# Cross-attention's output projections of eight tiles in pairs, by seven half products, in the turns after the batches are done

## The chip, the cores and the metric

The kernel runs on one core of a Trainium2 chip. The metric is device time of one execution in microseconds (us), lower is better; the median of several runs is given. PE is TensorE's matmuls, PEld its weight loads, DVE VectorE, ACT ScalarE, POOL GpSimd, SP the queue that issues the DMAs.

## The reference

One decoder block on x (8 batches x 224 tokens x 512) in float32, post-normalised, with a context of 8 x 750 x 384:

```python
x = layernorm(x + self_attention(x))        # 16 heads of 64
x = layernorm(x + cross_attention(x, ctx))  # below
x = layernorm(x + ffn(x))                   # ternary weights, inner 2048

# cross_attention
q, k, v = split(x @ Wq), split(ctx @ Wk), split(ctx @ Wv)
attn = softmax(q k^T * 64**-0.5)
out = merge(attn @ v)                       # 8 x 224 x 1024
return out @ Wo + bo                        # Wo: 1024 x 512
```

The change is in the last line alone: `out @ Wo`, a product of 1792 x 1024 by 1024 x 512, for 10 of its 14 tiles of 128 rows.

## The kernel before

x lies in SBUF as 14 tiles of 128 tokens x 512 (`x[0]` to `x[13]`). Three stages follow each other: self-attention to about 488 us of the span, cross-attention to about 1448, the feed-forward part to the end.

**Cross-attention** goes in 32 turns, `t` = 0 to 31, after a start turn -1. Eight turns make a group `p` of two batches (448 tokens); a turn takes four heads of one batch: `place(t)` gives group, head quarter `g` and batch `u`, odd turns are the second batch. So a group's tokens are complete, over all heads, at the end of the turn after its eighth. In a turn PE does, in this order:

1. `weighted(t - 1)`: softmax weights of the turn before times V (`ov_c`, L1383);
2. `scores(t)`: `sc_c` (L1253), 12 banks, in two halves `w` of two heads; ACT copies them out (L1235), DVE takes maxima (L1239);
3. `kv_steps(t, 1)` and `kv_steps(t + 1, 0)`, interleaved: V of this turn and K of the next (L1084, L1078);
4. `queries_opened` or `queries_closed`, the query products of the next pair of turns (L1091);
5. in some turns `cross_project` of the tiles that are complete: `project_out` (L264), eight matmuls of 128 x 128 by 128 x 512 into one bank (`mm_co`).

Beside this DVE finds each query's largest score in `maxima(w)` and subtracts it in `less_maxima` (L1355); ACT takes exponentials (L1367); POOL sums them for the denominators (`exponentials`, L1370 to L1372); DVE normalises the outputs of the turn before into `oT` (`normalise`, `coT`, L1326). `oT` is a ring of 512 tokens.

K, V and query products already use Strassen-Winograd: a product of 2 x 2 blocks by seven products of blocks instead of eight, with sums of blocks on POOL. Its sums of weights are prepared in self-attention in a tile `room` on POOL and stored to DRAM (`room_sums`, `room_query_sums`, called in self-attention turns 10 to 23), and are loaded again for each turn.

`done` says after which turn each tile's projection comes: tile 0 after turn 7, 1 and 2 after 8, 3 and 4 after 15, 5 and 6 after 16, 7 after 23, 8 and 9 after 24, the others after 31 and at the end. `cross_add` adds the bias on POOL (L1399), the bank on DVE (L1400), and takes the layernorm statistics.

The engines' order (PE, DVE, ACT, POOL) is the order in which the program calls them; each engine takes its instructions in that order and waits where a semaphore asks it to. SP's order is the scheduler's. Products take their PSUM banks from one pool of seven (`ps_mm`), in turn. The tiles of the pool `sb` have one buffer each unless `bufs` says otherwise: a new tile of a name waits until every reader of the one before is done. `w_t` has two; it takes the rounded weights of the feed-forward part on their way to DRAM in turns 12 to 23.

Of the kernel before, what the change touches and what calls it, by code (L numbers as in the profile page):

```python
# [21 lines left out]
F32 = mybir.dt.float32  # L22
BF16 = mybir.dt.bfloat16
AF = mybir.ActivationFunctionType
ALU = mybir.AluOpType
# [29 lines left out]
QG = HEADS // 4  # L55
EARLY = 7
CROWDED = 0, 7
LATE = 10
SOFTCLAMP = 50.0
SCALE = DH**-0.5  # L60
# [7 lines left out]
def decoder_block(ctx: ExitStack, tc: tile.TileContext, a: dict, out: bass.AP):  # L68
# [97 lines left out]
    def room_query_load():  # L166
        nc.sync.dma_start(
            out=room.rearrange("p (k n) -> p k n", k=KD),
            in_=a["xattn_Wq"].rearrange("(k p) n -> p k n", p=P),
        )  # L170

    def room_query_sums():

        blk = room.rearrange("p (h k g c n) -> p h c k g n", h=2, k=2, c=2, n=P)
        b = lambda h, c: blk[:, h, c]
        for n, y, p, q in (
            (0, b(0, 0), b(0, 1), b(0, 0)),
            (2, b(0, 1), b(1, 1), b(0, 1)),
            (1, b(1, 1), b(1, 1), b(0, 0)),
            (3, b(1, 0), b(1, 0), b(1, 1)),  # L180
        ):
# [5 lines left out]
    room_steps = room_sums(0), room_sums(1), room_query_sums()  # L187

    ident = const.tile([P, P], F32, name="ident")
    make_identity(nc, ident)  # L190
# [156 lines left out]
    with tc.tile_pool(name="a_sb", bufs=2) as sb, tc.tile_pool(  # L347
# [418 lines left out]
        for m in range(NS):  # L766
# [26 lines left out]
                next(room_steps[m // 15])  # L793
            if 20 <= m < 24:
                next(room_steps[2])
            next(sums)
            if m + 2 < NS:
                square_qk(m + 2)
# [36 lines left out]
                room_load(1)  # L835
            if m == 18:
                room_query_load()
            if m == NS - 3:
# [100 lines left out]
    with tc.tile_pool(name="c_sb", bufs=1, reuse_waits="tile") as sb, tc.tile_pool(  # L939
# [4 lines left out]
        ctx_odd = sb.tile([P, CTX], F32, name="ctx_odd")  # L944
        for b in range(1, B):
            open_context(b, (ctx_even, ctx_odd)[b % 2])
        xwo = load_w("xattn_Wo", INNER // P, DIM)
        load_context(1)
        nc.sync.dma_start(out=bo, in_=a["xattn_bo"].partition_broadcast(P))
        stage = sb.tile([P, 2, CHUNK], F32, name="w_stage")  # L950
# [445 lines left out]
            )  # L1396

        def cross_add(i):
            nc.gpsimd.tensor_tensor(x[i], x[i], bo, ALU.add)  # L1399
            nc.vector.tensor_tensor(x[i], outs.pop(i), x[i], ALU.add)  # L1400
            statistics(x[i], ln_mv[:, i, :], ln_ve[:, i, :])

        TURNS = B // 2 * 2 * QG
        jobs = {}
# [4 lines left out]
        for t, i0, i1 in ((18, 0, EARLY), (26, EARLY, LATE)):  # L1409
            job(t, roots, i0, i1)  # L1410
            n = t + 1
            for i in range(i0, i1):
                job(n, normalise_x, nc.gpsimd, i)
                n += 1
                job(n + (i == LATE - 1), largest_x, i)
            if i1 < LATE:
                job(n, row_scales, i0, i1)
        job(28, quantise_x, 0)
        job(29, quantise_x, 1)

        done = {}
        for i in range(NX):
            b = ((i + 1) * P - 1) // S
            t = 2 * QG * (b // 2 + 1) - 2 + b % 2
            done.setdefault(t + 1, []).append(i)

        kts, vs, outs = {}, {}, {}
        pTs = prior = None
        transpose_x(0)
        sum_x()  # L1430
        for n in range(2):
            stage_chunk(*chunks[n], n)
        for t in range(-1, TURNS):
# [3 lines left out]
            if t >= 0:  # L1437
                pTs = scores(t, copy if t else None)
                if t == 0:
                    weight_open(t)  # L1440
                nm = maxima(0)
                less_maxima(nm, pTs[0])
                if t == TURNS - 1:
                    for _ in normalise(t - 1, ov):
                        pass
                nm = maxima(1)
            ks = kv_steps(t + 1, 0) if t + 1 < TURNS else iter(())
            vals = kv_steps(t, 1) if t >= 0 else iter(())
# [313 lines left out]
```

## Time and profile before

| | |
|---|---|
| median of 3 runs | 1601.79 us (1601.24 to 1602.21) |
| profiled execution | 1601.96 us, span 1600.1 us |
| PE busy | 99% of the span |
| DVE, ACT, POOL busy | 83%, 62%, 61% |
| granted TensorE clock, mean | 0.999 |
| a turn of cross-attention without `mm_co` | mostly 26.3 us (even) or 27.0 us (odd) |
| `mm_co` of one tile on PE | 6.87 us |
| idle of PE that the list of waits names | 3.8 us in all |

Lines of the timeline read: start in us, length, engine, line of the kernel, operation, output <- inputs, shapes, how many instructions; in brackets the engine's idle time before it and what ended it. A float32 matmul is two instructions on PE. Matmuls are pipelined, so a group's length runs past the start of the next; the pitch is read from starts. Lines of a table by stretches read: from and to, length, busy time and count of PE, PEld, DVE, ACT and POOL, granted clock (1.00 is full), share of the DMA engines, GB/s.

### The profile page before, as it was taken

What the parts mean: (1) busy time and instruction counts of PE and PEld (TensorE: products, weight loads), DVE (VectorE), ACT (ScalarE), POOL (GpSimd) and SP (SyncE); (2) the same over time, 40 slices, a digit from 0 to 9 for tenths busy, and PEclk for the clock granted to TensorE, in tenths of its full rate; (3) what the DMA queues carried; (4) which work ended last, traced back from release to release, by engine and by line L of the source; (5) the groups of instructions that cost most, each with busy time, mean ns of one, the idle gap of its engine ahead of it and who ended that gap; (6) DMA issues with size and microseconds to landing.
All of it is one profiled execution on the core that took longest, in us unless ns stands there. A gap on an engine that the chain in (4) does not pass through costs nothing.

```text
span 1600.1 us, 27156 instructions
## 1 busy us (share of the span) xinstructions
PE 1589.1 (99%) x9684; PEld 1138.8 (71%) x9698; DVE 1323.8 (83%) x2809; ACT 996.9 (62%) x1858; POOL 972.6 (61%) x891
## 2 busy tenths in 40 slices
PE   9999999999999999999999999999999999999998
PEld 6677666667747888876888876788876888864443
DVE  3999897889966798886799876798887898978877
ACT  5667555656525777764668765687764666646663
POOL 5886565666524656685466785467686466753344
PEclk9999999999999999999999999999999999999999
DMA  8115342433204313241122252223240111213343
GB/s 302 47 53 198 90 129 85 139 89 119 83 20 162 105 59 100 66 159 54 60 67 80 85 181 64 73 81 118 79 162 24 34 40 38 73 54 97 64 90 106
DMA packets 143111, 149.14 MB, mean 93 GB/s; under 512 B 41088, under 2 KB 109184, under 8 KB 142592
## 3 DMA queue, kind: packets, MB, share of 16 engines
q1 hardware_dynamic: 142832, 147.40, 29.8%
q8 instruction: 77, 1.26, 0.3%
q14 instruction: 58, 0.48, 0.1%
q10 hardware_dynamic: 144, 0.00, 0.0%
HBM read 119.85 MB, written 18.87 MB: 87 GB/s over the span
## 4 chain that ended last, share of the span: by engine, by line
PE 94%; DVE 3%; ACT 2%; issue 1%; DMA 0%; POOL 0%; SPq 0%; POOLq 0%; ACTq 0%; DVEq 0%
PE sc_c L1253 10%; PE ov_c L1383 9%; PE v_x L1084 7%; PE k_x L1078 6%; PE mm_o L672 6%; PE mm_co L264 6%; PE mm_f L1558 5%; PE mm_v L547 5%; PE q_x L472 5%; PE v_w L1084 5%; PE k_w L1078 5%; PE mq_x L1091 3%; PE sc_a L574 3%; PE ov_a L643 3%; PE v_z L1084 3%; PE q_w L472 3%
## 5 line engine op out<-in xcount | busy, mean ns | idle before, releaser
L1370 POOL TENSOR_TENSOR csh<-cpT 125x672 f32<-125x672 f32 x128 | 209.8, 1639 | 109.8 <-DVE cpT L1355 94.0
L202 POOL TENSOR_TENSOR nm_i<-nm_q,mhalf 128x28 f32<-128x28 f32 x32 | 158.0, 4936 | 82.4 <-DVE nm_q L522 82.1
L1355 DVE TENSOR_TENSOR cpT<-cpT,mx_b 125x1344 f32<-125x1344 f32 x128 | 192.6, 1545 | 2.8
L1235 ACT COPY cpT<-sc_c 125x448 f32<-125x448 f32 x384 | 173.9, 566 | 18.3 <-PE sc_c L1253 14.1
L1367 ACT ACTIVATE cpT<-cpT 125x1344 f32<-125x1344 f32 x128 | 168.5, 1328 | 11.2 <-DVE cpT L1355 10.7
L1253 PE MATMUL sc_c<-cq,ckT 64*125 64x224 f32 x1536 | 162.2, 358 | 0.1
L1253 PEld LDWEIGHTS sc_c<-cq,ckT 64*125 64x125 f32 x1536 | 147.3, 184 | 14.4 <-issue 10.3
L1383 PE MATMUL ov_c<-cpT,cv 125*64 125x224 f32 x1536 | 152.9, 355 | 0.2 <-ACT cpT L1367 0.2
L1115 POOL TENSOR_TENSOR cv<-cv,cvmu 125x384 f32<-125x384 f32 x32 | 31.9, 998 | 191.5 <-ACT cv L1114 185.7
L1383 PEld LDWEIGHTS ov_c<-cpT,cv 125*64 125x64 f32 x1536 | 107.6, 137 | 44.9 <-issue 8.8
L547 PE MATMUL mm_v<-wv,xnT 128*128 128x512 f32 x224 | 100.4, 592 | 0.0
L1558 PE MATMUL mm_f<-ternary,xqT 128*128 128x512 bf16 x435 | 97.8, 379 | 0.7
L264 PE MATMUL mm_co<-xattn_Wo,coT 128*128 128x512 f32 x224 | 98.5, 593 | 0.0
L284 ACT ACTIVATE pr<-sc_a 128x448 f32<-128x448 f32 (+1 forms) x118 | 57.1, 535 | 60.3 <-PE sc_a L574 60.1
L1239 DVE TENSOR_TENSOR xw<-sc_c,cpT 125x448 f32<-125x448 f32 x64 | 39.6, 619 | 64.0 <-PE sc_c L1253 64.0
L1371 POOL TENSOR_TENSOR csm<-csh 125x224 f32<-125x224 f32 x128 | 85.1, 665 | 10.0
L1372 POOL TENSOR_TENSOR csm<-csm,csh 125x224 f32<-125x224 f32 x128 | 84.6, 661 | 10.0
L598 DVE TRANSPOSE_TENSOR_REDUCE sm_q<-pr 128x28 f32<-128x896 f32 x64 | 70.6, 1103 | 18.7 <-ACT pr L284 18.4
L1263 ACT COPY ov_s<-ov_c 128x448 f32<-128x448 f32 x31 | 16.5, 533 | 111.5 <-PE ov_c L1383 111.5
L672 PE MATMUL mm_o<-attn_Wo,oT 128*128 128x512 f32 x192 | 84.6, 593 | 0.0
L1558 PEld LDWEIGHTS <-xqT 128*128 128x128 bf16 x448 | 43.8, 98 | 53.2 <-issue 0.6
L264 PEld LDWEIGHTS mm_co<-xattn_Wo,coT 128*128 128x128 f32 x224 | 41.9, 190 | 47.9 <-issue 45.5
(240 smaller groups left out, 3992.7 us busy)
## 6 DMA issues: line engine op xcount, KB each, us to landing
w_slot<-qk_sums SPq DMA_DIRECT2D x22, 512.0 KB, 3.6
xw<-w_sums SPq DMA_DIRECT2D x32, 320.0 KB, 2.9
xwq<-xq_sums SPq DMA_DIRECT2D x16, 512.0 KB, 4.2
w_stage<-w_gateT SPq DMA_DIRECT2D x16, 512.0 KB, 5.5
w_stage<-w_upT SPq DMA_DIRECT2D x16, 512.0 KB, 5.3
w_stage<-w_downT SPq DMA_DIRECT2D x16, 512.0 KB, 4.4
tern<-w_t SPq DMA_DIRECT2D x24, 256.0 KB, 2.7
ternary<-tern SPq DMA_DIRECT2D x3, 2048.0 KB, 8.0
```

Source lines behind the costliest of these rows:

```text
L264: nc.tensor.matmul(mm, lhsT=oT[:, k, c : c + P], rhs=w[:, k, :], start=(k == 0), stop=(k == NPAIR - 1),)
L547: nc.tensor.matmul(mm, lhsT=xnT[:, k, at : at + P], rhs=wv[:, k, c * 512 : (c + 1) * 512], start=(k == 0), stop=(k == KD - 1),)
L672: nc.tensor.matmul(mm, lhsT=joint[g][:, hp, :] if at < 0 else o[:, at : at + P], rhs=wo[:, hp, :], start=(hp == 0), stop=(hp == NPAIR - 1),)
L1078: nc.tensor.matmul(mm, lhsT=w, rhs=c, start=start, stop=True, skip_group_check=True)
L1084: nc.tensor.matmul(mm[:, t, :], lhsT=c[:, t * CT : (t + 1) * CT], rhs=w, start=start and t == 0, stop=True, skip_group_check=True,)
L1235: nc.scalar.copy(pT[:, j, 2 * c2 : 2 * c2 + 2, :], banks[c2][j])
L1253: nc.tensor.matmul(sc[j][:, i, :], lhsT=kT[h0 : h0 + DH, w, ct * CT : (ct + 1) * CT], rhs=cq[h0 : h0 + DH, t % 2, w], start=True, stop=True,)
L1355: nc.vector.tensor_tensor(pT[:, j], pT[:, j], nm[:CT, j] .rearrange("p (o q) -> p o q", o=1) .to_broadcast([CT, NCT, S]), ALU.add,)
L1367: nc.scalar.activation(pT[:, j], pT[:, j], AF.Exp)
L1370: nc.gpsimd.tensor_tensor(half, pT[:, j, 0:3], pT[:, j, 3:6], ALU.add)
L1383: nc.tensor.matmul(ov[h0 : h0 + DH, w, :], lhsT=v[:, ct, hq * DH : (hq + 1) * DH], rhs=pTs[w][:, j, ct, :], start=(ct == 0), stop=(ct == N ...
L1558: nc.tensor.matmul(mm, lhsT=xqTs[i][:, k, :], rhs=w[:, k, cols], start=(k == 0), stop=(k == KD - 1),)
```

## The change

Tiles 0 to 9 are no longer projected when they are complete but one to two turns later, in turns 9, 17 and 25. `PAIRED` names them by turn: pair (0, 1) and tile 2; pairs (3, 4) and (5, 6); pair (7, 8) and tile 9. Each pair is a product of 256 x 1024 by 1024 x 512, taken in two halves of 256 columns `s`; each half is 2 x 2 blocks (128 rows, 512 of the inner dimension, 128 columns) and goes by seven products of blocks, each four matmuls with 128 columns. The first half of the columns stands behind the scores, ahead of `maxima(1)` in DVE's queue; the second at the end of the turn, behind the queries and the third exponential, ahead of the fourth.

`sum_out` makes the sums of the activations on POOL (three operations of 512 columns in the first half, of which S3 replaces a block of `oT`, two in the second), into two `w_t` tiles. `out_pair` does the products; partial results go through ACT into `cku4` and `cvu2`, buffers that `kv_steps` uses too, and are added to x on DVE (from PSUM) and POOL (from SBUF). `out_single` does a single tile in a half of 256 columns. The weights' half is loaded by `load_out(s)`: two blocks and four sums, 2 MB, the other half as soon as one has been used; after turn 25 the whole weight, for the tiles 10 to 13, which stay as they were. The sums of weights are made in self-attention turns 25 to 28 in `room`. The bias is added ahead, at the end of turns 4 to 6, 12 to 15 and 20 to 22; the statistics come at the end of turns 9, 17, 25.

```diff
+PAIRED = ((0, 1), (2,)), ((3, 4), (5, 6)), ((7, 8), (9,))
+    def room_out_load():
+        nc.sync.dma_start(
+            out=room.rearrange("p (k n) -> p k n", k=NPAIR),
+            in_=a["xattn_Wo"].rearrange("(k p) n -> p k n", p=P),
+        )
+    def room_out_sums():
...
+        for n, y, p, q in (
+            (0, b(0, 0), b(0, 1), b(0, 0)),
+            (2, b(0, 1), b(1, 1), b(0, 1)),
+            (1, b(1, 1), b(1, 1), b(0, 0)),
+            (3, b(1, 0), b(1, 0), b(1, 1)),
+        ):
+            for i in range(2):
+                nc.gpsimd.tensor_tensor(y[:, i], p[:, i], q[:, i], ALU.subtract)
+                nc.sync.dma_start(out=sums_xo[:, i, n], in_=y[:, i])
+            yield
...
-        xwo = load_w("xattn_Wo", INNER // P, DIM)
+        def load_out(s):
+            src = a["xattn_Wo"].rearrange("(k p) n -> p k n", p=P)
+            if s is None:
+                nc.sync.dma_start(out=xwo, in_=src)
+                return
+            for c in range(2):
+                at = (2 * s + c) * P
+                nc.sync.dma_start(
+                    out=xo[:, 2 * c : 2 * c + 2].rearrange("p h k n -> p (h k) n"),
+                    in_=src[:, :, at : at + P],
+                )
+            nc.sync.dma_start(out=xo[:, 4:], in_=sums_xo[:, s])
+        load_out(0)
...
+        def sum_out(pair, s):
+            (a11, _), (a21, a22) = (out_blocks(i) for i in pair)
+            s1, s2 = sums_o[pair] = [
+                sb.tile([P, CHUNK], BF16, name="w_t", bufs=2)
+                .bitcast(F32)
+                .rearrange("p (k n) -> p k n", n=P)
+                for _ in range(2)
+            ]
+            if s == 0:
+                nc.gpsimd.tensor_tensor(a21, a11, a21, ALU.subtract)
+            nc.gpsimd.tensor_tensor(s2, a22, a21, ALU.subtract)
+            nc.gpsimd.tensor_tensor(s1, s2, a11, ALU.add)
+        def out_product(mm, c, w, start):
+            for k in range(4):
+                nc.tensor.matmul(
+                    mm, lhsT=c[:, k], rhs=w[:, k], start=start and k == 0, stop=True,
+                    skip_group_check=True,
+                )
+        def out_pair(pair, s, following):
...
+            parts = sb.tile([P, HALF + 9], F32, name="cku4")
+            m1, u2, u4 = (parts[:, i * P : (i + 1) * P] for i in range(3))
+            w0 = sb.tile([P, HALF + 9], F32, name="cvu2")[:, :P]
...
+            out_product(x_, a11, b11, True)
+            nc.scalar.copy(m1, x_)
+            out_product(z_, a12, b21, True)
+            plus(nc.vector, c11, z_)
+            out_product(x_, s2, t2, False)
+            nc.scalar.copy(u2, x_)
+            nc.gpsimd.tensor_tensor(s2, a12, s2, ALU.subtract)
+            out_product(w_, s3, t3, True)
+            nc.scalar.copy(w0, w_)
+            out_product(x_, s1, t1, False)
+            nc.scalar.copy(u4, x_)
+            plus(nc.gpsimd, c11, m1)
+            out_product(w_, a22, t4n, False)
+            plus(nc.vector, c21, w_)
+            out_product(x_, s2, b22, False)
+            plus(nc.vector, c12, x_)
+            if following:
+                sum_out(following, s)
+            for y, q in ((c22, w0), (c22, u4), (c21, u2)):
+                plus(nc.gpsimd, y, q)
+        def out_single(i, s):
+            mm = ps_mm.tile([P, 2, P], F32, tag="mm", name="co_m")
+            for h, c in enumerate(out_blocks(i)):
+                for k in range(4):
+                    nc.tensor.matmul(
+                        mm, lhsT=c[:, k], rhs=xo[:, h : 4 : 2, k, :],
+                        start=(h == 0 and k == 0), stop=(h == 1 and k == 3),
+                    )
+            y = x[i][:, 2 * s * P : 2 * (s + 1) * P]
+            nc.vector.tensor_tensor(y, mm.rearrange("p c n -> p (c n)"), y, ALU.add)
+        def out_half(p, s):
+            tiles = PAIRED[p]
+            pairs = [t for t in tiles if len(t) == 2]
+            for n, t in enumerate(tiles):
+                if len(t) == 1:
+                    out_single(t[0], s)
+                    continue
+                out_pair(t, s, pairs[n + 1] if n + 1 < len(pairs) else None)
+            if p < 2 or s == 0:
+                load_out(1 - s)
+            else:
+                load_out(None)
...
+        for p, tiles in enumerate(PAIRED):
+            for n, i in enumerate(i for t in tiles for i in t):
+                job(2 * QG * p + QG + n, add_bias, i)
...
-            done.setdefault(t + 1, []).append(i)
+            if b // 2 == B // 2 - 1:
+                done.setdefault(t + 1, []).append(i)
...
                 nm = maxima(0)
                 less_maxima(nm, pTs[0])
...
+                p = t // (2 * QG) - 1
+                out_turn = t % (2 * QG) == 1 and p >= 0
+                if out_turn:
+                    sum_out(PAIRED[p][0], 0)
+                    out_half(p, 0)
                 nm = maxima(1)
...
             for _ in query:
                 pass
+            if out_turn:
+                sum_out(PAIRED[p][0], 1)
+                out_half(p, 1)
             for _ in rest:
                 pass
             if t >= 0:
                 exponentials(t, 1, pTs[1], (1,))
...
+            if out_turn:
+                out_statistics(p)
```

More of the change, by code (lines that the diff above doesn't have):

```diff
@@ L185, in room_query_sums @@
             yield
-    room_steps = room_sums(0), room_sums(1), room_query_sums()
+    sums_xo = dram.tile([P, 2, 4, NPAIR // 2, P], F32, name="xo_sums")
+    def room_out_load():
[4 more added lines that the diff above has]
+    def room_out_sums():
+        blk = room.rearrange("p (h k s c n) -> p h c s k n", h=2, k=4, s=2, c=2, n=P)
+        b = lambda h, c: blk[:, h, c]
+        for n, y, p, q in (
[8 more added lines that the diff above has]
+            yield
+    room_steps = room_sums(0), room_sums(1), room_query_sums(), room_out_sums()
     ident = const.tile([P, P], F32, name="ident")
@@ L795, in decoder_block @@
                 next(room_steps[2])
+            if 25 <= m < 29:
+                next(room_steps[3])
             next(sums)
@@ L837, in decoder_block @@
                 room_query_load()
+            if m == 23:
+                room_out_load()
             if m == NS - 3:
@@ L946, in decoder_block @@
             open_context(b, (ctx_even, ctx_odd)[b % 2])
-        xwo = load_w("xattn_Wo", INNER // P, DIM)
+        xwo_all = wpool.tile([P, INNER // P * DIM], F32, tag="w", name="xattn_Wo")
+        xwo = xwo_all.rearrange("p (k n) -> p k n", n=DIM)
+        xo = xwo_all.rearrange("p (b k n) -> p b k n", b=8, n=P)
+        def load_out(s):
[11 more added lines that the diff above has]
+        load_out(0)
         load_context(1)
@@ L1398, in cross_add, with out_blocks @@
         def cross_add(i):
-            nc.gpsimd.tensor_tensor(x[i], x[i], bo, ALU.add)
+            add_bias(i)
             nc.vector.tensor_tensor(x[i], outs.pop(i), x[i], ALU.add)
             statistics(x[i], ln_mv[:, i, :], ln_ve[:, i, :])
+        def out_blocks(i):
+            at = i * P % RING
+            return [oT[:, 4 * h : 4 * h + 4, at : at + P] for h in range(2)]
+        sums_o = {}
+        def sum_out(pair, s):
[10 more added lines that the diff above has]
+            nc.gpsimd.tensor_tensor(s1, s2, a11, ALU.add)
@@ new lines, in out_product @@
+        def out_product(mm, c, w, start):
[5 more added lines that the diff above has]
+        def out_pair(pair, s, following):
+            (a11, a12), (s3, a22) = (out_blocks(i) for i in pair)
+            s1, s2 = sums_o.pop(pair)
+            b11, b21, _, b22, t1, t2, t3, t4n = (xo[:, i] for i in range(8))
+            c11, c12, c21, c22 = (
+                x[i][:, (2 * s + c) * P : (2 * s + c + 1) * P]
+                for i in pair for c in range(2)
+            )
+            parts = sb.tile([P, HALF + 9], F32, name="cku4")
+            m1, u2, u4 = (parts[:, i * P : (i + 1) * P] for i in range(3))
+            w0 = sb.tile([P, HALF + 9], F32, name="cvu2")[:, :P]
+            x_, z_, w_ = (
+                ps_mm.tile([P, P], F32, tag="mm", name=f"co_{n}") for n in "xzw"
+            )
+            plus = lambda eng, y, q: eng.tensor_tensor(y, q, y, ALU.add)
+            out_product(x_, a11, b11, True)
[18 more added lines that the diff above has]
+                plus(nc.gpsimd, y, q)
@@ new lines, in out_single @@
+        def out_single(i, s):
[5 more added lines that the diff above has]
+                        start=(h == 0 and k == 0), stop=(h == 1 and k == 3),
+                    )
+            y = x[i][:, 2 * s * P : 2 * (s + 1) * P]
+            nc.vector.tensor_tensor(y, mm.rearrange("p c n -> p (c n)"), y, ALU.add)
@@ new lines, in out_half, with add_bias @@
+        def out_half(p, s):
[10 more added lines that the diff above has]
+                load_out(None)
+        def add_bias(i):
+            nc.gpsimd.tensor_tensor(x[i], x[i], bo, ALU.add)
@@ L1403, in decoder_block, with out_statistics @@
+        def out_statistics(p):
+            for t in PAIRED[p]:
+                for i in t:
+                    statistics(x[i], ln_mv[:, i, :], ln_ve[:, i, :])
         TURNS = B // 2 * 2 * QG
@@ L1424, in decoder_block @@
             t = 2 * QG * (b // 2 + 1) - 2 + b % 2
-            done.setdefault(t + 1, []).append(i)
+            if b // 2 == B // 2 - 1:
+                done.setdefault(t + 1, []).append(i)
         kts, vs, outs = {}, {}, {}
         pTs = prior = None
+        out_turn = False
         transpose_x(0)
```

## The prediction

> **What bounds the kernel now.** I read the page first: busy shares, then the chain that ended last.
>
> ```profile
> PE 1589.1 (99%) x9684; PEld 1138.8 (71%) x9698; DVE 1323.8 (83%) x2809; ACT 996.9 (62%) x1858; POOL 972.6 (61%) x891
> ...
> PE 94%; DVE 3%; ACT 2%; issue 1%; DMA 0%; POOL 0%; SPq 0%; POOLq 0%; ACTq 0%; DVEq 0%
> ```
>
> TensorE is the bound and the chain is nearly all its own work. The list of waits agrees: PE's waits in the whole span sum to 3.8 us (1.2, 0.9, 0.8, 0.7, 0.2). So every matmul removed is worth its length, and every wait put in front of PE is paid in full. Second, PE's timeline over the end of turn 8 and turn 9 of cross-attention:
>
> ```profile
> 746.79 13.90 PE L264 MATMUL mm_co<-xattn_Wo,coT 128*128 128x512 f32 x32
> 760.62 4.76 PE L1383 MATMUL ov_c<-cpT,cv 125*64 125x224 f32 x48
> 765.31 5.03 PE L1253 MATMUL sc_c<-cq,ckT 64*125 64x224 f32 x48
> 770.27 0.92 PE L1084 MATMUL v_x<-xw,ctx_odd 128*125 128x128 f32 x6
> ...
> 771.66 1.47 PE L1084 MATMUL v_z<-xw,ctx_odd 128*125 128x128 f32 x12
> 772.97 1.43 PE L1078 MATMUL k_z<-ctx_even,xw 128*128 128x375 f32 x4
> ...
> 786.79 0.92 PE L1091 MATMUL mq_x<-xwq 128*128 128x224 f32 x4
> 787.64 0.41 PE L1383 MATMUL ov_c<-cpT,cv 125*64 125x224 f32 x2
> ```
>
> Starts give the pitch (the durations overlap): 32 output-projection instructions take 760.62 - 746.79 = 13.83 us, 0.432 each; twelve 128-column ones 772.97 - 771.66 = 1.31 us, 0.109 each. The turn runs value products, scores, key/value steps, query products, next turn, without a hole. Third, POOL at the end of the same turn:
>
> ```profile
> 779.16 1.64 POOL L1370 TENSOR_TENSOR csh<-cpT 125x672 f32<-125x672 f32 x1 [3.21 <-DVE cpT L1355]
> ...
> 787.99 0.66 POOL L1219 TENSOR_TENSOR cq<-cq,cvmu 128x224 f32<-128x224 f32 x1
> 788.61 1.64 POOL L1370 TENSOR_TENSOR csh<-cpT 125x672 f32<-125x672 f32 x1
> 790.33 0.67 POOL L1371 TENSOR_TENSOR csm<-csh 125x224 f32<-125x224 f32 x1
> 791.08 0.66 POOL L1372 TENSOR_TENSOR csm<-csm,csh 125x224 f32<-125x224 f32 x1
> 791.82 1.64 POOL L1370 TENSOR_TENSOR csh<-cpT 125x672 f32<-125x672 f32 x1
> ```
>
> Of POOL's lines from the first one here on (others left out) only that one shows an idle time: from 779.16 POOL works back to back, and it is done with the third exponential sum at 791.74, 4.1 us after PE has ended the queries (787.64). In turns 17 and 25 the same difference is 4.1 and 4.0 us. POOL is late at each turn's end; today nothing on PE asks for it there.
>
> **PE's own work.** Removed: ten tiles' projections, six stretches of the chain, 6.97 + 13.73 + 13.73 + 13.73 + 6.87 + 13.73 = 68.8 us. Added: four pairs, two halves, seven products of four matmuls of 128 columns, each two instructions: 448 x 0.109 = 48.9 us (6.12 a half pair). Tiles 2 and 9 in halves of 256 columns: 64 instructions at 0.216 (between 0.190 for 224 columns, the pitch of the mq products, and 0.315 for 375) = 13.8 us. PE saves 6.0 us; I give back 0.9 for six starts (v_x takes 0.76 us for six where 0.65 is due).
>
> **The sums at the turn's end.** The second half of each eighth turn starts with `sum_out` on POOL, behind the third exponential sum. A 512-column add takes 1.27 us (L1399). With T the end of the queries on PE, POOL comes free at T + 4.1. The first half moves PE, ACT and POOL of this turn together, except that the first exponential no longer waits 0.19 us for VectorE: T + 3.9. S2 is there at T + 5.2. PE has two products that need no sum (A11 B11, A12 B21): 1.75 us. It then waits 3.5 us, with ~0.1 for the hand-over, and behind it stand the rest of the half pair, the single tile and the whole next turn. Three turns: 10.5 us. S1 follows in time.
>
> In the first half the same operations find POOL idle: without `mm_co` turn 9 starts at 746.9 in the clock above, scores end 9.7 us later at 756.6, the product with S2 comes at 758.4, with S1 at 760.1. POOL ends turn 8's last sum at 754.0 and the three 512-column operations by 757.8, S2 at 756.5. Nothing waits.
>
> **Turn 17, two pairs.** Before the second pair PE needs M1 copied out, and ACT's copy goes into the buffer (`cku4`) that POOL must have read for the first pair. POOL reads it last, after `sum_out` of the second pair, and before that POOL adds M1 to C11, which waits for VectorE. VectorE stands in `less_maxima`:
>
> ```profile
> 1013.25 0.92 PE L1084 MATMUL v_x<-xw,ctx_odd 128*125 128x128 f32 x6
> ...
> 1019.04 3.02 DVE L1355 TENSOR_TENSOR cpT<-cpT,mx_b 125x1344 f32<-125x1344 f32 x2
> ```
>
> In that clock: VectorE free 1022.1, its add (0.27, from 0.377 at 224 columns) 1022.4, POOL's add 1022.9, three sums 1026.7, three 128-column adds 1028.1, ACT's copy and hand-over 1028.5. A 128-column POOL add is not in the trace; I take 0.46, on the line through 0.665 (224) and 1.27 (512), between 0.24 (a 64-column copy) and 0.67. PE, from 1013.3, has used up the first pair and two products at 1021.2. Wait: 7.2 us (6.4 to 8.0). In the second half the first pair waits 3.5 as elsewhere; for the second, the sums may only be written when the first pair's last product has read the buffer (two `w_t`): two sums 2.5, three adds 1.4, copy 0.4, less 1.75 of cover: 2.7 us (2.1 to 3.3). Turn 17 adds 9.9.
>
> **The clock.** A TensorE at rest is slow afterwards:
>
> ```profile
> 1.15 3.79 PE L737 MATMUL ov_a<-ones 128*128 128x128 f32 x16 [1.15 <-POOL ones L196]
> ...
> 7.43 2.89 PE L418 MATMUL mm_qk<-xnT,wq 128*128 128x128 f32 x24 [0.70 <-DVE xnT L398]
> ...
> 1595.00:1600.10 5.10, 0.00 (x0) 0.00 (x0) 1.57 (x5) 0.00 (x0) 0.78 (x1) 0.76 0.27 103
> ```
>
> At the start 16 instructions of 128 columns take 3.6 us (0.22 each); from 7.43 on 24 take 2.73 (0.114). At the end (third line: span, five engines, granted clock 0.76) the last matmul ends near 1593.7; 0.24 x 5.1 x 2 = 2.4 us at half speed mean that the clock halved near 1597.7, 3.9 us after. The wait of 7.2 us is longer, so the next matmuls run at half: 5.6 us at the start (1.15 to about 6.7), which costs half of it, 2.8. I take 2.5, between 0 and 2.8; the waits of 3.5 and 2.7 us lie under 3.9 and cost nothing more.
>
> The Trainium skill ("TensorE: Matmul & The Clock Gate", the HAM clock gate) speaks against such a change: no idle gaps over about 3 us, since one idle window of about 3.4 us halves the clock until some 3.4 us of work have passed. By that the 7.2 would cost 1.7 to 3.4 us, and the waits of 3.5 us could, by luck of the window, cost that too. At the end of this trace it took 3.9 us.
>
> **What hides the rest.**
> - Preparing the weight sums: eight 512-column operations at 1.32 us (L183) on POOL in self-attention turns 25 to 28, two each: 2.6 us into idle times of 4.93, 4.33, 4.34 and 3.47 us before `nm_i`. Uncovered 10.5 us. Their eight 256 KB stores and the 2 MB load pass SP as the query sums' did four turns earlier: 0.
> - Loads of the halves: six of 2 MB behind PE's last reads on SP. The two blocks have 512-byte rows like w_slot<-attn_Wq (256 KB in 2.7 us): at most 10.8 us, while 17.4 us of key, value and query products lie between the halves. 0; uncovered, what exceeds 17.4. The blocks for the next turn's V are queued behind the first half's load but wait for V products of this turn anyway.
> - ACT's copies (0.27 of 128 columns, from 0.35 at 224) lie under products of 0.87. In the first half M1's copy stands behind the evictions (771.7), done by 772.0, needed at 772.1.
> - Queued behind the new VectorE adds are `maxima(1)` and its exponentials: in turns 9 and 25 1.3 us late, PE 9.6. Bias adds move into POOL's 17 us idle. Statistics (1.0 each) move to the end of the turn: VectorE is free 5.9 to 6.7 us into the next one, first needed at 6.4: 0 to 0.3 in turn 18.
> - The ends of turns 7, 8, 15, 16, 23, 24 become like others, 26.3 and 27.0 us long without holes: 0.
>
> **Sum.** -6.0 + 0.9 + 10.5 + 9.9 + 2.5 = +17.8 us on an execution of 1601.96 (span 1600.1 and 1.9 around it): 1619.8, or 1619.6 on the median of 1601.79. By the page alone it would be 17.0 to 18.7.
>
> **Rivals.**
> A. Turn 17's second pairs run free, because the reading adds end earlier than the queue lets me believe: 9.9 and 2.5 fall away, +5.4, 1607.2. Against: the copy waits for the third of those adds, and POOL takes its queue in order. 0.10.
> B, faster. The sums are never late: POOL would have to reach `sum_out` by T + 0.5 instead of T + 3.9, since PE's cover is 1.75 and a sum 1.27. Then -6.0 + 0.9: 1596.7 (it decides from an average wait under 0.6 us over the eight half pairs). Against: POOL has no hole in 12.6 us. 0.05.
> C. The clock halves in the three waits of 3.5 us too, which lie close to 3.9: +7.5, 1627.1. 0.13.
> D. Part of it: waits just eat the saving, within 3.2 us of 1601.8. 0.03.
> The forecast itself: 0.69, from 1615 to 1622 by its bounds (clock 0 to 2.8, 0.8 and 0.6 in turn 17, 0.3 on each 3.5).
>
> The measurement tells about 0.2% (3.2 us) from no change: faster 0.05 (B), same 0.03 (D), slower 0.92. The range, 1610 to 1628, takes in the forecast and C and goes part of the way to A, whose chain could be partly hidden; it leaves out A, B and D, 0.18.
>
> **What would show it.** In the profile after, PE should have waits at `out_product`: three of about 3.5 us on POOL's S2, in turn 17 one near 7.2 and one near 2.7 on ACT's M1 copy; the chain should hold POOL for about 1%, and in POOL's timeline the sum S2 should start where the third exponential sum ends, about 4 us after the last query product. Matmuls after the 7.2 us should show a granted clock under 1. I am wrong if PE's waits sum to under 11 us, if 128-column products have a pitch other than 0.109, or if a load ends a wait.

## The result: 20 us slower, and the profile after

The changed kernel takes 1621.6 us (median of 4 executions, 1620.35 to 1623.23); the kernel before, timed with it, 1601.7 us (1601.24 to 1602.21). The ratio is 1.0125, with a 95% interval of 1.0107 to 1.0142: 19.9 us. The prediction was 1619.6 us. The profiled execution took 1621.66 us, with a span of 1619.9; the steps below are set against the span before, 1600.1, a difference of 19.8 us.

Two lines of the page after, busy times (instructions behind the x) and the chain that ended last:

```profile
PE 1590.3 (98%) x10036; PEld 1175.1 (73%) x10050; DVE 1326.6 (82%) x2827; ACT 1004.9 (62%) x1890; POOL 1032.6 (64%) x959
...
PE 86%; DVE 6%; POOL 4%; ACT 3%; issue 1%; DMA 0%; POOLq 0%; SPq 0%; DVEq 0%; ACTq 0%
```

PE is busy 1.2 us longer than before, although its products would take about 4 us less at full speed (there are more instructions, but narrower ones): part of them ran at half speed. And the chain, which was PE's for 94%, is PE's for 86%. The list of waits of PE after (total us, times, longest) says where it left PE:

```profile
PE co_x L1471 <- POOL w_t L1466: 9.3, 3, 3.1
PE co_x L1471 <- ACT cku L1493: 8.2, 2, 6.9
PE q_x L496 <- ACT qm L322: 1.2, 4, 0.4
...
PE mm_f L1717 <- DVE x L1446: 0.9, 1, 0.9
```

Three waits for the sum S2 that POOL makes (L1466), two for ACT's copy of M1 (L1493): 17.5 us that were not there before. The other two lines are small, but one is new (`mm_f`) and one has grown from 0.9; I come back to both.

The first wait, in turn 9. PE's timeline, then the chain in order of time (start, length, what), then POOL's timeline:

```profile
776.83 1.05 PE L1471 MATMUL co_x<-xattn_Wo,coT 128*128 128x128 f32 x8
777.72 1.06 PE L1471 MATMUL co_z<-xattn_Wo,coT 128*128 128x128 f32 x8
781.86 1.16 PE L1471 MATMUL co_x<-xattn_Wo,w_t 128*128 128x128 f32 x8 [3.08 <-POOL w_t L1466]
```

```profile
764.96 1.32 PE v_w L1130 x12
...
771.20 0.96 POOL cv L1175
...
779.94 0.65 POOL csm L1418
780.59 1.23 POOL w_t L1466
781.82 0.04 issue
781.86 1.16 PE co_x L1471 x8
```

```profile
779.94 0.65 POOL L1418 TENSOR_TENSOR csm<-csm,csh 125x224 f32<-125x224 f32 x1
780.55 1.26 POOL L1466 TENSOR_TENSOR w_t<-coT 128x512 f32<-128x512 f32 x1
```

The chain shows more than the idle time does. From 768 us on it runs along POOL's queue: two sets of exponential sums, a key and a value step, two query additions, the third set, and only then S2. With queries done at 776.8, POOL gets to S2 3.7 us later. The wait is put down to one 1.26 us addition, but it is the length of the queue in front of it. That is why POOL has 4% of the chain, where I had looked only at the wait and written 1%.

The long wait, in turn 17's first half, and what follows it, on PE, then POOL and ACT at the same time, then busy times by stretches (the figure ahead of the last two is the granted clock):

```profile
995.45 1.06 PE L1471 MATMUL co_z<-xattn_Wo,coT 128*128 128x128 f32 x8
1003.38 2.08 PE L1471 MATMUL co_x<-xattn_Wo,w_t 128*128 128x128 f32 x8 [6.87 <-ACT cku L1493]
1005.24 1.91 PE L1471 MATMUL co_w<-xattn_Wo,coT 128*128 128x128 f32 x8
1006.95 1.91 PE L1471 MATMUL co_x<-xattn_Wo,w_t 128*128 128x128 f32 x8
...
1032.85 2.08 PE L1471 MATMUL co_x<-xattn_Wo,w_t 128*128 128x128 f32 x8 [3.13 <-POOL w_t L1466]
```

```profile
997.32 0.45 POOL L1491 TENSOR_TENSOR x<-cku,x 128x128 f32<-128x128 f32 x1 [4.75 <-DVE x L1491]
997.73 1.26 POOL L1465 TENSOR_TENSOR coT<-coT 128x512 f32<-128x512 f32 x1
999.07 1.26 POOL L1466 TENSOR_TENSOR w_t<-coT 128x512 f32<-128x512 f32 x1
...
1002.16 0.86 POOL L1491 TENSOR_TENSOR x<-cku,x 128x128 f32<-128x128 f32 x2
```

```profile
1003.06 0.27 ACT L1493 COPY cku<-co_x 128x128 f32<-128x128 f32 x1 [9.82 <-POOL x L1491]
```

```profile
1000.00:1005.00 5.00, 1.62 (x7) 1.63 (x8) 0.00 (x0) 0.27 (x1) 2.87 (x5) 0.50 0.00 0
1005.00:1010.00 5.00, 5.00 (x30) 5.00 (x29) 0.10 (x1) 0.80 (x3) 2.59 (x4) 0.60 0.00 0
...
780.00:785.00 5.00, 3.14 (x28) 3.14 (x29) 0.00 (x0) 0.69 (x3) 4.84 (x6) 1.00 0.00 0
```

POOL's row reads as predicted: 4.75 us behind VectorE, three sums, the reading additions, and then ACT may copy M1. Behind the wait, eight 128-column instructions take 1.7 to 1.9 us instead of 0.89, at a granted clock of 0.50 to 0.60. The product at 1032.85 is slow too (2.08), though its wait was 3.13 us; after the equally long wait at 781.86 the clock stayed at 1.00.

With the starts of the turns on PE, before and after: turns 7 to 9 together +1.8 us, 15 to 17 +14.0, 23 to 25 +2.7: +18.5. The cross-attention stage starts 0.56 us later, and its end, from the last turn to the first gate product, takes 1.05 us more.

### The profile page after: what moved, and what is told of

Same layout as the page of the kernel before. It is cut to its first block, busy times and chain, and to the rows that moved or that the text cites. A ratio compares the mean times of both kernels' runs of the same rounds, so it can differ in the third digit from the quotient of the medians.

```text
span 1619.9 us, 28061 instructions
## 1 busy us (share of the span) xinstructions
PE 1590.3 (98%) x10036; PEld 1175.1 (73%) x10050; DVE 1326.6 (82%) x2827; ACT 1004.9 (62%) x1890; POOL 1032.6 (64%) x959
## 4 chain that ended last, share of the span: by engine, by line
PE 86%; DVE 6%; POOL 4%; ACT 3%; issue 1%; DMA 0%; POOLq 0%; SPq 0%; DVEq 0%; ACTq 0%
PE sc_c L1299 9%; PE ov_c L1429 9%; PE v_x L1130 6%; PE mm_o L696 6%; PE k_x L1124 6%; PE mm_f L1717 5%; PE mm_v L571 5%; PE v_w L1130 5%; PE q_x L496 5%; PE k_w L1124 4%; PE mq_x L1137 3%; PE v_z L1130 3%; PE sc_a L598 2%; PE k_z L1124 2%; PE ov_a L667 2%; PE q_w L496 2%
## 5 line engine op out<-in xcount | busy, mean ns | idle before, releaser
L1413 ACT ACTIVATE cpT<-cpT 125x1344 f32<-125x1344 f32 x128 | 168.8, 1329 | 11.3 <-DVE cpT L1401 10.8
L1130 PEld LDWEIGHTS v_x<-xw,ctx_even 128*125 128x125 f32 x480 | 60.9, 187 | 17.0 <-issue 3.9
L571 PEld LDWEIGHTS mm_v<-wv,xnT 128*128 128x128 f32 x224 | 42.5, 190 | 42.1 <-issue 41.3
L1130 PEld LDWEIGHTS v_x<-xw,ctx_odd 128*125 128x125 f32 x480 | 61.1, 187 | 16.2 <-issue 4.6
```

Of the source, the lines that this page charges most:

```text
L571: nc.tensor.matmul(mm, lhsT=xnT[:, k, at : at + P], rhs=wv[:, k, c * 512 : (c + 1) * 512], start=(k == 0), stop=(k == KD - 1),)
L1130: nc.tensor.matmul(mm[:, t, :], lhsT=c[:, t * CT : (t + 1) * CT], rhs=w, start=start and t == 0, stop=True, skip_group_check=True,)
L1413: nc.scalar.activation(pT[:, j], pT[:, j], AF.Exp)
```

## The experiments

Times are medians beside the kernel before on the same chip (1601.7 to 1601.9 us in all of them); the changed kernel's 1621.6 is the result above and was not taken again beside them. "Turn" lengths are starts of the value products on PE. The theory: PE does save its few microseconds; what is lost is waiting for POOL's queue, in turn 17 also for a shared buffer, and the slow clock behind the waits. S1 and S2 are the sums that POOL makes, M1 is the first product, which ACT copies out. The rivals: moving and splitting the projections costs by itself; loads; VectorE held back.

**Sums made early, turns 9 and 25.** The second half's sums move from the turn's end to just behind the first half.

```diff
                     out_half(p, 0)
+                    if p != 1:
+                        sum_out(PAIRED[p][0], 1)
...
-                sum_out(PAIRED[p][0], 1)
+                if p == 1:
+                    sum_out(PAIRED[p][0], 1)
                 out_half(p, 1)
```

> Only in turns 9 and 25, the sums S1 and S2 for the second half are made right behind the first half instead of at the turn's end behind the third exponential sum; everything else is as in the changed kernel (1621.6 us). Theory (PE waits there for POOL's place in its queue): the two waits of 3.08 us before the product with S2 vanish, 3.25 each with the hand-over, turns 9 and 25 fall from 49.9 and 50.3 to 46.7 and 47.0, total -6.5, 1615.1 us (1614.0 to 1616.2). Rival (the loss lies in splitting and moving, the wait only takes the place of queueing elsewhere in the turn): turns as long as before, total 1621.6, a new wait of about 3 us at another line. Rival (the early sums make the exponentials' sums late): total between, with PE waiting at ov_c.

Measured: 1615.2 us (ratio 1.0084, 1.0071 to 1.0098), 6.4 less than the changed kernel. Turn 9 falls from 49.90 to 46.55, turn 25 from 50.27 to 46.88. Of the three waits on S2 one is left, turn 17's:

```profile
PE co_x L1471 <- ACT cku L1493: 8.2, 2, 6.9
PE co_x L1471 <- POOL w_t L1466: 3.1, 1, 3.1
```

POOL's place in the queue is the cause, and nothing else in those turns becomes late.

**One more addition in the queue.** The same cause doubled from the other side: an unused 512-column addition on POOL ahead of the second half's sums.

```diff
+                more = sb.tile([CT, NCT // 2, S], F32, name="csh")
+                more = more.rearrange("p c n -> p (c n)")[:, :DIM]
+                nc.gpsimd.tensor_tensor(
+                    more, x[PAIRED[p][0][0]][:CT], x[PAIRED[p][0][1]][:CT], ALU.add
+                )
                 sum_out(PAIRED[p][0], 1)
```

> The changed kernel plus one unused 512-column addition on POOL ahead of the second half's sums, in turns 9, 17 and 25. Theory (POOL's queue sets the waits): each wait of 3.1 us grows by 1.27 to about 4.35, +3.8; and at that length the clock halves behind all three (it did behind 3.88 us in the run with own buffers, and behind 3.1 in some places and not in others), 1.5 to 2.8 us each where the profile after paid 1.7 for one of the three: together 1627 to 1632 us. Rival (the clock's loss doesn't depend on the wait's length): +3.8, 1625.4. Rival (PE's waits are not set by POOL's queue): 1621.6.

Measured: 1631.9 us (1.0186, 1.0169 to 1.0203), 10.3 more than the changed kernel for 3.8 us of POOL's work. The waits grow as they should:

```profile
PE co_x L1471 <- POOL w_t L1466: 13.3, 3, 4.4
PE co_x L1471 <- ACT cku L1493: 8.2, 2, 6.9
```

13.3 - 9.3 = 4.0. The other 6.3 us are the clock: it now halves behind all three, 2.3 to 2.9 us each, where the changed kernel's profile has 1.7 behind one of them (turn 9 grows by 3.9, of which 1.3 is wait).

**Turn 17: the buffer alone.** The second pair's copied products get a buffer of their own, idle until later turns.

```diff
+            if pair == PAIRED[1][1]:
+                own = quant.tile([P, DIM], F32, name="xq_r")
+                m1, u2, u4, w0 = (own[:, i * P : (i + 1) * P] for i in range(4))
+            else:
...
```

> Only the second pair of turn 17 gets its own buffer for the copied products (M1, U2, U4, W0), so ACT's copy of its M1 need not wait for POOL's reading adds of the first pair; POOL's order stays. Theory (two things in series, the buffer and behind it POOL's place in the queue): in the first half the wait of 6.87 us becomes a wait for S2, made by POOL from 999.07 to 1000.33 in the profile after, where PE has been idle since 996.4: 4.0 us are left, -3.0; in the second half the wait of 1.33 us goes, -1.5; total 1617.1, and up to 2.8 less (1614.3) if a wait of 4 us leaves the clock full. Rival (the buffer alone holds it): both waits and the slow clock go, -11.3, 1610.3. Rival (POOL's queue alone): no change, 1621.6.

Measured: 1619.0 us (1.0110, 1.0096 to 1.0124). Turn 17 falls from 68.53 to 63.85, 4.7 for the 4.5 of the theory: the wait on M1's copy is gone and a wait on S2 stands in its place, as said.

```profile
1000.50 2.08 PE L1471 MATMUL co_x<-xattn_Wo,w_t 128*128 128x128 f32 x8 [3.88 <-POOL w_t L1466]
```

The total fell by only 2.6 and missed the 1617.1 of the theory: in the profiled execution the clock was also halved behind turn 25's unchanged wait (51.76 us for 50.27).

**Turn 17: buffer and order.** POOL's addition of M1, which waits for VectorE, is put behind the next pair's sums.

```diff
-            plus(nc.gpsimd, c11, m1)
...
-            for y, q in ((c22, w0), (c22, u4), (c21, u2)):
+            for y, q in ((c11, m1), (c22, w0), (c22, u4), (c21, u2)):
                 plus(nc.gpsimd, y, q)
```

> As the run with the second pair's own buffer, and POOL's add of M1 to C11 is put behind the sums of the following pair, so that POOL makes these without waiting for VectorE. Theory: both waits of turn 17's second pairs and the half clock behind the first go: -7.0 - 1.5 - 2.8 = -11.3, 1610.3 us (1608.5 to 1612); turn 17 falls from 68.5 to about 57.2 if the wait of 3.1 us at its end leaves the clock full. Rival (order does nothing, the buffer does all): the same time as the run with the buffer alone. Rival (VectorE held back is what counts): 1617 or more, PE waits for S2.

Measured: 1613.9 us (1.0072, 1.0058 to 1.0086; single executions from 1612.4 to 1615.2). Turn 17 is 57.73 us long, 10.8 less, where the theory said 11.3; both second-pair waits are gone but for 0.3 us. The total missed its bounds by 1.9 us, and the reason is on PE's timeline of this kernel in turn 9, where the change does nothing:

```profile
777.64 1.06 PE L1471 MATMUL co_z<-xattn_Wo,coT 128*128 128x128 f32 x8
781.80 2.08 PE L1471 MATMUL co_x<-xattn_Wo,w_t 128*128 128x128 f32 x8 [3.10 <-POOL w_t L1466]
783.67 1.70 PE L1471 MATMUL co_w<-xattn_Wo,coT 128*128 128x128 f32 x7
```

The same wait of 3.1 us as at 781.86 in the changed kernel, but the products behind it run at half speed: turn 9 takes 52.66 us here, 49.90 there, and turn 25 takes 51.75 for 50.27. (This profile is of the slowest of the five executions. Their mean granted clocks go with their times: 0.997 at 1612.4 and 1612.7 us, 0.996 at 1613.9, 0.995 at 1615.2.) Over the profiled executions of this kernel, the changed one, the first and the third run above, which have such waits left, and the next, there are 13 waits of 3.1 us; the clock was halved behind 9 of them, at 1.4 to 2.9 us each, 1.8 in the mean. By place it is 1 of 4 in turn 9, 5 of 5 in turn 17's second half and 3 of 4 in turn 25. So it is not the same chance everywhere, and what decides stays open.

**The wait filled.** Six unused products on PE in turn 17's long wait.

```diff
+            if s == 0 and pair == PAIRED[1][1]:
+                idle = ps_mm.tile([P, DIM], F32, tag="mm", name="co_idle")
+                for k in range(6):
+                    nc.tensor.matmul(
+                        idle, lhsT=a12[:, 0], rhs=xwo[:, k, :], start=True, stop=True,
+                    )
             out_product(x_, s2, t2, False)
```

> The changed kernel plus six unused products of 512 columns (0.86 us each, 5.2 us) on PE inside turn 17's wait of 6.87 us, ahead of the product with S2 of the second pair; what they compute is not used. They take no time of the path, since PE stands idle there for 6.87 us. Theory (the clock is halved by the idle time): the products behind it run at 0.893 us per eight instead of 1.7 to 1.9, -2.8, 1618.8 us (1617.8 to 1620). Rival (the products behind the wait are slow for another reason, such as operands that come late or a busy memory): 1621.6, same pitch of 1.7 to 1.9 us.

Measured: 1620.2 us (1.0115, 1.0100 to 1.0130; 1619.1 to 1622.0). PE's timeline of this kernel:

```profile
996.13 5.32 PE L1499 MATMUL co_idle<-xattn_Wo,coT 128*128 128x512 f32 x12
1003.16 1.16 PE L1471 MATMUL co_x<-xattn_Wo,w_t 128*128 128x128 f32 x8 [1.72 <-ACT cku L1493]
1004.16 1.06 PE L1471 MATMUL co_w<-xattn_Wo,coT 128*128 128x128 f32 x8
1005.05 1.06 PE L1471 MATMUL co_x<-xattn_Wo,w_t 128*128 128x128 f32 x8
```

The products behind run at their full pitch, and turn 17 falls by 2.92 us (65.61 for 68.53), for the 2.8 expected: work that nobody uses makes the kernel faster there. Idle time, not operands, halves the clock. The total fell by 1.4 and just missed its bounds. It is no measure of the filling: in the profiled execution turn 25 paid 1.6 for its own wait, behind which the clock had stayed full in the changed kernel's profile, and the wait of 0.89 us at the stage's end (`mm_f`) is absent, which is worth 1.05; the last experiments come back to that.

**Halves without sums.** Each tile by itself, in the same turns and halves, with the same loads; no sums of activations, no copied products.

```diff
-                out_pair(t, s, pairs[n + 1] if n + 1 < len(pairs) else None)
+                for i in t:
+                    out_single(i, s)
...
-                    sum_out(PAIRED[p][0], 0)
-                sum_out(PAIRED[p][0], 1)
```

> The changed kernel with every tile projected by itself: same turns, same halves, same loads and preparation of the weight sums, but eight 256-column products per tile and half and no sums of activations, no copied products. Theory (only the waits and the clock behind the sums cost): 320 instructions x 0.216 = 69.1 us in place of 68.8, +0.3; +0.8 in the self-attention stage, where the profile after shows the preparation's additions on POOL beside VectorE; up to +0.9 at the stage's end, so 1602.8 to 1603.7 us, no wait of PE at these products. Rival (moving to turns 9, 17, 25 or splitting in halves costs by itself): 1606 or more.

Measured: 1602.4 us (1.0004, 0.9995 to 1.0014), 0.7 more than before, 0.4 under the theory's bounds and far from the rival's 1606. PE's timeline shows 48 instructions back to back, 10.45 us in starts (0.218 each), no wait behind:

```profile
777.59 10.52 PE L1518 MATMUL co_m<-xattn_Wo,coT 128*128 128x256 f32 x48
788.04 1.17 PE L1429 MATMUL ov_c<-cpT,cv 125*64 125x224 f32 x10
```

Moving, splitting and reloading the weights cost next to nothing.

**The preparation alone.** The kernel before plus the load and the eight additions in self-attention, their results unused.

```diff
+            if 25 <= m < 29:
+                next(room_steps[3])
...
+            if m == 23:
+                room_out_load()
```

> The kernel before plus only the preparation: the 2 MB load and the eight additions on POOL with their stores in turns 25 to 28 of self-attention; the projections stay as before and the sums are not used. The prediction put this at 0. Theory (POOL's additions slow VectorE's scaling beside them, L537, from 1.34 to 2.35 and 2.65 us for two, and so the copies that PE waits for): +0.8, 1602.5 us (1602.1 to 1602.9), the start of cross-attention moved by 0.8 and VectorE's scaling again near 2.3 to 2.7 in four turns. Rival (the shift comes from elsewhere in the change): 1601.7.

Measured: 1602.0 us (1.0001, 0.9992 to 1.0010): +0.3, which the total can't tell from 0 or from 0.8. The timeline can: set against the kernel before, self-attention's turns begin 0.58 us earlier until 392 us (a start-up difference, between -0.6 and +0.5 over all these profiles) and 0.22 later from 421 on. So 0.8 us are lost between, in this kernel as in the changed one. VectorE's scaling in the kernel before, then in the changed one:

```profile
389.66 1.34 DVE L537 SCALAR_TENSOR_TENSOR qk<-qk,gscale,sq_qk 128x448 f32<-128x448 f32 x2
400.81 1.78 DVE L537 SCALAR_TENSOR_TENSOR qk<-qk,gscale,sq_qk 128x448 f32<-128x448 f32 x2
```

```profile
389.42 2.35 DVE L561 SCALAR_TENSOR_TENSOR qk<-qk,gscale,sq_qk 128x448 f32<-128x448 f32 x2
401.57 2.65 DVE L561 SCALAR_TENSOR_TENSOR qk<-qk,gscale,sq_qk 128x448 f32<-128x448 f32 x2
```

In three of the four turns two scalings take about 1 us longer beside POOL's two additions. In the fourth the additions start after the scaling (430.67 in the changed kernel), and the scaling takes 1.66 us for 1.65 before. The chain through ACT comes late, and PE waits for ACT's copy (the fourth wait of `q_x`).

**All sums early.** Both cures, and turn 17's second-half sums early as well, in four small buffers that are idle then.

```diff
                     out_half(p, 0)
+                    sum_out(PAIRED[p][0], 1, p == 1)
...
-                sum_out(PAIRED[p][0], 1)
                 out_half(p, 1)
...
+            if apart:
+                parts = [quant.tile([P, KD, P], BF16, name="xqT", bufs=3) for _ in "abc"]
...
+                s1, s2 = sums_o[pair] = parts[:2], parts[2:]
+                for k in range(2):
+                    b = slice(2 * k, 2 * k + 2)
+                    nc.gpsimd.tensor_tensor(s2[k], a22[:, b], a21[:, b], ALU.subtract)
```

> Both cures together: sums of every second half made right behind the first half (in turn 17 in four small buffers, in halves of two blocks each), the second pair of turn 17 with its own buffer and its sums ahead of the add that waits for VectorE. Theory (the waits and the clock behind them are all that is lost): 1621.6 - 3 x 3.25 - 7.0 - 1.5 - 2.8 - 1.7 (the half clock behind the wait in turn 17's second half) = 1598.8 us (1597.3 to 1600.8), below the kernel before (1601.7) by the 4.9 us that PE saves less about 1.4 around the stage; no wait of PE at the products, TensorE's clock 0.99 or more. Rival (splitting into halves and narrow products costs as much as the products save): 1601.7 or more without any wait shown. Rival (something else is late next, such as a load or the exponentials): waits of PE of other names, 1600 to 1610.

Measured: 1599.5 us (0.9986, 0.9977 to 0.9995), in 11 executions from 1599.0 to 1600.3: 2.2 us faster than before and 22.1 than the changed kernel. Of PE's waits at the products, 0.5 us in all are left:

```profile
PE mm_f L1743 <- DVE x L1446: 0.9, 1, 0.9
...
PE co_x L1490 <- POOL w_t L1525: 0.3, 1, 0.3
...
PE co_x L1490 <- POOL w_t L1485: 0.2, 1, 0.2
```

The three groups of turns take 1.5, 1.8 and 0.7 us less than before, 4.05 together. That is the saving of the products, with the 0.5 us of waits still in it. The executions are close together again (1.3 us from first to last, 2.9 in the changed kernel). The spread goes with the clock: in the changed kernel its mean is 0.996 in the fastest execution and 0.994 in the slowest, here 0.999 or 1.000 in all.

**The additions behind the scaling.** A copy of one column, which waits for VectorE's scaling, ahead of the preparation's additions.

```diff
             if 25 <= m < 29:
+                scaled = sb.tile([P, 1], F32, name="scaled")
+                nc.gpsimd.tensor_copy(scaled, qk[m + 1][:, 1, G - 1 : G])
                 next(room_steps[3])
```

> The run with all sums early (1599.5) plus one copy of a single column on POOL ahead of the preparation's additions in self-attention turns 25 to 28, which waits for VectorE's scaling, so that the additions no longer run beside it. Theory (POOL's additions slow VectorE's scaling beside them and with it the chain that PE waits for): the scaling takes 1.3 to 1.8 us for two again, and the 0.8 us between 392 and 421 us fall away, 1598.7 us. Rival (the additions cost by POOL's lateness at the key norms, not beside VectorE): the shift stays or grows, 1599.5 or more, since the additions now start 1 us later.

Measured: 1598.7 us (0.9980, 0.9971 to 0.9989): -0.8. VectorE and POOL in this kernel:

```profile
389.25 1.35 DVE L561 SCALAR_TENSOR_TENSOR qk<-qk,gscale,sq_qk 128x448 f32<-128x448 f32 x2
400.51 1.64 DVE L561 SCALAR_TENSOR_TENSOR qk<-qk,gscale,sq_qk 128x448 f32<-128x448 f32 x2
```

```profile
390.73 0.19 POOL L822 COPY scaled<-qk 128x1 f32<-128x1 f32 x1 [1.21 <-DVE qk L561]
390.87 2.51 POOL L207 TENSOR_TENSOR w_room<-w_room 128x512 f32<-128x512 f32 x2
394.50 4.82 POOL L226 TENSOR_TENSOR nm_i<-nm_q,mhalf 128x28 f32<-128x28 f32 x1 [1.11 <-DVE nm_q L546]
```

The scaling is as fast as before, the additions are faster too (2.51 for 3.27), and POOL, which starts them later, still idles 1.11 us before it is needed. The turns at 392 and 421 us have the same shift against before (-0.43): the loss was the company, not the work.

**The end of the stage.** Three more result buffers, taken and given back unused, alone and together with the run above:

```diff
                 out_statistics(p)
+                if p == 2:
+                    for _ in range(3):
+                        ps_mm.tile([P, P], F32, tag="mm", name="co_free")
```

> The run with all sums early (1599.5) plus three result buffers taken and given back unused after turn 25, so that the order in which the seven PSUM buffers come round at the stage's end is that of the kernel before (18 + 3 = 21 more than before, three times seven). Theory (the wait of 0.89 us of the first gate product on VectorE's last additions comes from the buffer that it happens to get): the wait goes, -0.9 to -1.05, 1598.5 us. Rival (VectorE is really late at the stage's end): the wait stays, 1599.5.

> All sums early, the free buffers and the additions after the scaling together. Theory: 1599.5 - 0.95 - 0.8 = 1597.7 us (1597.2 to 1598.3), 4.0 below the kernel before: what the seven products save without a wait. Rival (one of the two small losses is noise): 1598.5 to 1598.7.

Measured: 1599.4 and 1598.7 us; the wait of 0.89 us stays in both. The theory said 1598.5 and 1597.7: a miss. As far as these runs show, buffers that no instruction touches don't take a turn in the rotation. Buffers in use do move the wait: every run with 28 result buffers for the ten tiles has it, while the halves without sums (20) and the filled wait (29) don't. So three small unused products, each into a buffer of its own, in place of the unused buffers (with the run of 1598.7 as the base):

```diff
+                    for _ in range(3 if p == 2 else 0):
+                        free = ps_mm.tile([P, P], F32, tag="mm", name="co_free")
+                        a1, _ = out_blocks(PAIRED[p][0][0])
+                        nc.tensor.matmul(
+                            free, lhsT=a1[:, 0], rhs=a1[:, 1], start=True, stop=True,
+                        )
```

> The run with all sums early and the additions behind the scaling (1598.7) plus three unused products of 128 columns on PE in turn 25 (0.33 us), each into a result buffer of its own; unused buffers alone had changed nothing. Theory (the first gate product waits 0.89 us because the last buffer of the output projections is the one that it gets, and buffers come round in order of real use): the wait goes, -0.9 + 0.3 = -0.6, 1598.1 us (1597.8 to 1598.5). Rival (the wait is tied to VectorE's last additions whatever the buffer): +0.3, 1599.0.

Measured: 1598.3 us (0.9978, 0.9969 to 0.9987); the wait is gone from PE's list. The time fell by 0.3 rather than 0.6, because turn 25 grew by 0.7 instead of 0.3. This is the fastest version of the study, 3.5 us under the kernel before.

## Why the prediction was right, and where by luck

The forecast, that the sums come late behind POOL's queue, is what happened. Its sum of +17.8 stands against +19.8, but not every term held:

| term | predicted | measured (us) |
|---|---|---|
| PE's own work, six starts in it | -5.1 | -4.05 (all sums early, 0.5 of waits in it) |
| three waits for S2 | 3 x 3.5 | 3 x 3.25 |
| turn 17, second pairs | 7.2 + 2.7 | 7.0 + 1.5 |
| clock | 2.5 | 2.8 behind the long wait, 1.7 behind one of 3.1 |
| preparation | 0 | 0.8 |
| end of the stage | 0 | 1.05 |

(The measured terms add to 20.6. Start-up takes 0.24 of it back. The other 0.5 is the size of the waits inside the -4.05, which the changed kernel doesn't have; that they account for it is not shown.)

- **Waits for S2: right.** POOL came free at T + 3.7 (I wrote T + 3.9), S2 was there at T + 5.0 (5.2), PE's cover 1.79 (1.75). The run with early sums takes exactly these waits away, the run with one more addition lengthens them.
- **Turn 17's first half: right, link by link.** VectorE's add, POOL's add, three sums, three small additions, copy: 7.0 for 7.2, a 128-column addition on POOL 0.45 for my interpolated 0.46. The two runs on turn 17 show that buffer and order are two locks in series: the first alone turns 7.0 us into 4.0, both together into none.
- **Turn 17's second half: size off.** I let both sums wait for the first pair's last product, and the copy for both. POOL's rows show S2 starting at 1037.50, 0.74 us after its last operation, well before that last product: the new S2 goes where the old S1 lay, which is read two products earlier. Hence 1.5 for 2.7. I had not followed which of the two buffers each sum gets.
- **Clock: the step that failed.** "The waits of 3.5 and 2.7 us lie under 3.9 and cost nothing more." The 3.9 came from one place, the end of the kernel, and I used it as a threshold. It is none: 3.1 us of waiting halved the clock in 9 of 13 places. So rival C, to which I gave 0.13, is true in part in each of the five profiles, at 9/13 x 1.8 = 1.2 us for each wait rather than its 2.5. In the changed kernel's own profile it is one of the three. The Trainium skill ("TensorE: Matmul & The Clock Gate", Part 1) describes a free-running window of about 3.4 us and warns in its last table of gaps over about 3 us. The runs go under the figure of Part 1: a wait of 3.1 us was enough in 9 places. That equal waits have unequal effects would fit a window that runs freely, but no run here shows windows.
- **Products: mis-sized by 1.1.** Eight 128-column instructions take 0.893 us, 0.1116 each, not 0.109: the row I used (`v_x`, `v_z`) has 125 weight columns, `co_x` has 128. 448 of them take 50.0 us in place of 48.9. With that 1.1 my -5.1 becomes -4.0. The run with all sums early shows -4.05, but with 0.5 us of waits in it, so PE's own saving is nearer 4.5 and the close match is partly luck. A pitch other than 0.109 was one of my three signs of being wrong, and by its letter it came true.
- **Preparation: the cover was there, the price was not 0.** POOL's idle time did hide the additions from POOL's own deadline. What I left out is VectorE, working beside them; 0.8 us, and gone when they start behind its scaling.
- **End of the stage: not seen.** 28 result buffers in place of ten shift which buffer the first gate product gets; it got one that VectorE's last additions still had to read.
- **Loads, bias additions, statistics, halves: 0, right.** No wait of PE in any run was ended by a load of halves, and the halves without sums cost 0.7 us, preparation included.

So the total was closer than its terms: the waits came out 2.2 us shorter than written, and clock, products, preparation and the end 4.9 us longer. That these nearly cancel is luck.

## What to carry to other kernels

An engine that is nowhere near the bound by its busy share (POOL: 61%) can still be full for the ten microseconds that count: before giving it work, follow its queue back from the moment when the result is needed, and put the work where its row shows idle time (here 2.2 and 2.9 us behind the first half, in the same turn). Where a saving is 4 us and a wait costs 3 plus the slow clock behind it, less work on the bound is worth nothing unless every operand is there in time; the same seven products lost 20 us and then won 3.5 with little but the order and the buffers changed. When a wait is found, ask for the next lock behind it before counting its whole length as gain.

## What the runs showed of the hardware that I had not expected

- **The clock can halve behind waits of 3.1 us, and need not.** It did in 9 of 13 places; behind waits of 3.9 to 6.9 us it halved in all 7 that the profiles show, behind waits of 1.3 to 1.7 us in none of 5. The price behind 3.1 us is 1.4 to 2.9 us. One kernel's executions differ by up to 3 us, and their granted clocks with them; a profile shows one execution. Granted clock by stretches in the run with one more addition, behind its waits of 4.4 us in turns 9 and 25:

```profile
785.00:790.00 5.00, 5.00 (x31) 5.00 (x30) 0.16 (x1) 1.63 (x4) 2.59 (x4) 0.62 0.00 0
...
1285.00:1290.00 5.00, 4.30 (x20) 4.30 (x21) 0.00 (x0) 0.53 (x2) 3.74 (x5) 0.50 0.01 3
```

- **VectorE and POOL slow each other.** Two scalings with two SBUF inputs take 2.35 to 2.67 us instead of 1.34 to 1.78 beside two 512-column additions on POOL, and these 3.27 instead of 2.51. The Trainium skill ("SBUF — State Buffer", SBUF: two separate sides) says that a VectorE operation with two SBUF inputs and a GpSimd operation that reads SBUF exclude each other for a whole instruction. The growth by about 1 us on one side and 0.8 on the other fits that, though no run here shows the lock itself; VectorE's transposes beside the additions kept their 1.10 us.
- **A result buffer that no instruction uses did not take its turn**: three unused ones left the wait of 0.89 us, three in use took it away. The unused ones stood at the end of turn 25, the used ones in its middle; that the place makes no difference is not shown.
